# Raw rows by feature for the key and query products, a reordered first gather, and on-chip node sums for the last chunk of a graph-transformer layer

## The chip, the cores and the metric

The kernel runs on one core of a Trainium2 chip. The metric is device time in microseconds (us) of one execution. A core has TensorE (PE: matmuls, with the weight loads PEld beside them), VectorE (DVE), ScalarE (ACT), GpSimd (POOL), SyncE (SP), and 16 DMA engines. SP, ACT and POOL issue DMAs, each from its own in-order instruction queue. All data is 32-bit float, and in the trace each 128x512 product is two matmul instructions.

## The reference, cut to what matters

N = 10,000 nodes with D = 512 features, 160,000 edges sorted by destination, 8 heads of 64.

```python
xn = layernorm(x)
gnn = relu(segment_sum((xn @ W)[src] * edge_w[:, None], dst) + bias)
q, k, v = split(xn @ w_qkv.T)
q = softmax(q, over the 64 of a head) / 8 ; k = softmax(k, over all nodes)
mix = gamma_layernorm(((k^T v per head) applied to q) @ w_out.T)
x = x + gnn + mix
x = x + experts(layernorm(x))      # 2-matmul FFN, hidden 6*341, top-2 router on the mean row
```

## The kernel before, in words

The nodes are cut into `NCH` = 20 chunks: 19 of 512 rows (128 partitions x `SUB` = 4) and a last one of 272 rows (68 x 4). There are four stages.

**Early stage (0 to 160 us, chunks 0 and 1).** `normal_rows` (L411) loads each chunk of x on SP (L416), takes row statistics on DVE (`row_stats`, L166 and L167) and 1/std on POOL (L169, L171), normalises on ACT (L422) and writes the result to `xn_d` in HBM on ACT's queue (L424). The first two chunks stay in SBUF (`KEPT`), the others go through 7 buffers. After `LISTS` = 10 chunks the edge lists are loaded (L446 to L451), and from then on two steps of `place_edges` (L454 on, all on DVE) run for each chunk normalised. Meanwhile PE does the key and query products of chunks 0 and 1 (`times`, L209), into which `work` (L698) threads more `normal_rows`.

**Keys stage (160 to 1236 us, chunks 2 to 19).** For each chunk: `turned_rows` (L837) turns the normalised rows with 16 PE transposes (`transposed`, L201) that ACT and DVE copy out of PSUM (L203) into `xnT`, which has one buffer; DVE forms four sums `xs_b` (L226 to L229); `seven` (L246, its products at L243) makes keys and queries by a seven-product scheme; ACT takes exponents (L896 to L901), scaled by `usable` (1.0 while the weights are small enough); DVE does the query softmax (L192 to L194); PE adds keys^T times rows into the context (`pc`, L911) and turns the queries (L201), which ACT writes to HBM. The rows for `pc` are read back from `xn_d` by SP (L834).

**Edges, threaded through the keys and the attention stage.** Edges lie in 1250 tiles of 128. For each tile POOL gathers the 128 source rows by an indirect DMA into one of 24 `msg` buffers (L583). Tiles go in 217 groups (`NQ`), of 8 tiles and later of 4. A visit of a group (`edges_summed`, L595) is 16 or 8 matmul instructions with a 0/weight matrix (L601), an ACT copy (L604), and a write of partial node sums to `part_d` in HBM (L605). `work(us)` adds a model cost and visits groups up to that cost divided by `PACE`. The stage starts at minus 16 tiles' worth (L862). `carry` (L673) joins neighbouring windows in HBM by an accumulating DMA on POOL. `gathered(c)` (L1013) gathers chunk c's node sums from `part_d`, forcing enough groups first (`far_enough`, `AT_HAND`).

**Attention stage (1297 to 2143 us).** For each chunk: queries times mix (`po`, L209), layer norm, 16 transposes of the node sums `at` (L201) into `aT`, and the product with the graph weights (`pg`, L209), with bias and relu on DVE (L1089, L1090). PE's order is written out by hand. At chunk 17 (`c == NCH - 3`) `all_edges_in` visits the last six groups, carries, and gathers the sums of chunks 18 and 19; then come `po` of chunk 19 and `pg` of 17, 18 and 19.

**Experts stage (2143 us to the end).** The FFN (L243) over 20 chunks. Its first product needs rows of chunk 0 read back (L328), normalised (ACT L351), turned (DVE L367) and summed (`xs`, L233 to L236). `sums_of_weights` (L226 to L229 on 1280 elements) prepares its weights in chunk 17.

Of the kernel before, what the change touches and what calls it, by code (L numbers as in the profile page):

```python
# [17 lines left out]
P = 128  # L18
# [11 lines left out]
ROWS_IN = 1.6  # L30
LISTS = 10
# [6 lines left out]
MIXED = 3  # L38

AT_HAND = [(5, 320), (7, 384), (8, 424), (9, 472), (10, 520), (11, 560), (12, 604), (13, 640), (14, 680), (15, 716), (16, 752),  # L40
           (17, 788), (18, 820)]
# [13 lines left out]

@with_exitstack
def gps_layer_kernel(
    ctx: ExitStack,
    tc: tile.TileContext,
    x: bass.AP,  # L60
    src: bass.AP,
# [40 lines left out]

    const = ctx.enter_context(tc.tile_pool(name="const", bufs=1))
# [33 lines left out]
    stats2 = const.tile([P, NCH, SUB, 2], F32, name="stats2")  # L137

# [10 lines left out]
    ZERO_ROW = NQ * P  # L149
# [38 lines left out]
    def softmax_rows(q, r, s):  # L188

        q3 = q[:r, s, :].rearrange("p (h e) -> p h e", e=HEAD)  # L190
        qs = small.tile([P, D // HEAD], F32, name="qs")
        nc.vector.tensor_reduce(qs[:r], q3, axis=AX.X, op=ALU.add)  # L192
        nc.vector.reciprocal(qs[:r], qs[:r])
        nc.vector.tensor_tensor(q3, q3, qs[:r, :, None].to_broadcast([r, D // HEAD, HEAD]), ALU.mult)  # L194
# [29 lines left out]
    def sums_of(o, a11, a12, a21, a22):  # L224
# [4 lines left out]
        nc.vector.tensor_tensor(o[3], a12, o[1], ALU.subtract)  # L229
# [149 lines left out]
    def sums_of_weights():  # L379
        w1_sb, w1_sum = held_w["w1"], held_w["w1_sum"]  # L380
        p_half, q_half = slice(0, PAIRS * P), slice(PAIRS * P, 2 * PAIRS * P)
        sums_of([w1_sum[:, i] for i in range(4)], w1_sb[:, :KH, p_half], w1_sb[:, KH:, p_half],
# [5 lines left out]
    with ExitStack() as ph:  # L388
# [17 lines left out]

        normal = []
        placing = []
        last_stats = [None]

        def normal_rows(n):  # L411

            for c in range(len(normal), min(len(normal) + n, NCH)):
                r = chunks[c][1]
                xt = (xp if c < KEPT else a_io).tile([P, SUB, D], F32, name="xn")
                nc.sync.dma_start(xt[:r], tokens(x, c))  # L416
                mv = small.tile([P, SUB, 2], F32, name="mv")
# [10 lines left out]
                for _ in range(2 if placing else 0):  # L428
                    next(placing[0], None)
# [3 lines left out]
        nc.scalar.dma_start(part_d[ZERO_ROW : ZERO_ROW + P, :], zero)  # L433
        normal_rows(2)
# [8 lines left out]
        n_odd = ep.tile([1, 1], I32, name="n_odd")  # L443

# [9 lines left out]
        def place_edges(dst_sb, row_sb):  # L454


            nc.vector.tensor_scalar(row_sb, row_sb, 2, None, op0=ALU.arith_shift_right)
            yield
# [40 lines left out]
            nc.vector.scalar_tensor_tensor(place, place, float(SUB), good, op0=ALU.add, op1=ALU.subtract)  # L499
            yield  # L500
# [23 lines left out]
        def window_at(node, more):  # L524
            tile_no = NET * (node / N) ** 0.5 + more
            return min(max(int(tile_no / 2 if tile_no < 2 * PAIRED else tile_no - PAIRED), 0), NW)

        def span(c):
            return window_at(chunks[c][0], -SPARE), window_at(chunks[c][0] + SUB * chunks[c][1], SPARE)

        def spans_hold():
            for c, (b, r) in enumerate(chunks):
                for i, w, op, edge in ((0, span(c)[0], ALU.is_le, b), (1, span(c)[1], ALU.is_ge, b + SUB * r)):
                    at = 3 + len(AT_HAND) + 2 * c + i
                    nc.vector.tensor_scalar(count[:, at : at + 1], bases[:, w : w + 1], float(edge // SUB), None, op0=op)
# [37 lines left out]
        def edges_in(i):  # L573
# [4 lines left out]
            for j in range(batch):  # L578
                for h in range(GROUP):
                    k = h * batch + j  # L580
                    if k < n:
                        m[k] = pools["m"].tile([P, D], F32, name="msg")
                        nc.gpsimd.indirect_dma_start(  # L583
# [11 lines left out]
        def edges_summed(i, batch, m, sel):  # L595
# [7 lines left out]
            part = pools["w"].tile([P, D], F32, name="part")  # L603
            nc.scalar.copy(part, pm)  # L604
            nc.scalar.dma_start(part_d[i * P : (i + 1) * P, :], part)  # L605
# [5 lines left out]

        def squares_of(w, tag):
            sq = b_io.tile([P, KB, D], F32, name="sq", tag=tag)
            nc.scalar.activation(sq, w, AF.Square)
            return sq
# [19 lines left out]
        def oddities():  # L635
# [8 lines left out]
            nc.vector.tensor_tensor(n_odd, n[:, 0:1], n[:, 1:2], ALU.add)  # L644

# [30 lines left out]
        carried = []  # L676
        for i in range(PARTS):
# [7 lines left out]
        ahead = [AHEAD]  # L685
        EARLY_TOTAL = PRODUCT * KB * ROWS_IN * 3 * KB

# [10 lines left out]
        def work(us):  # L698
# [6 lines left out]
            edges_to(groups_of(int(done[1] / pace[0])))  # L705

        in_order = ph.enter_context(ExitStack())
        in_order.enter_context(tc.manual_schedule(engines={mybir.EngineType.PE}))
# [11 lines left out]
        def all_edges(fp):  # L720
# [12 lines left out]
            nc.vector.tensor_copy(row_of, four)  # L733
            dst_sb = fp.tile([P, NET], I32, name="dst_far")
# [95 lines left out]
        def rows_of(c):  # L830
# [3 lines left out]
            nc.sync.dma_start(xn[: chunks[c][1]], tokens(xn_d, c))  # L834
            return xn

        def turned_rows(c, xn):  # L837
            xnT = b_io.tile([P, KB, SUB * P], F32, name="xnT")
            transposed(xnT, xn, chunks[c][1], psum, "ps", by_act=range(KB) if c < EARLY else (1, 3))
            return xnT  # L840

        def finish(o, ek, r, at):
            if o is ek:
                nc.vector.tensor_tensor(kacc[:r], kacc[:r], ek[:r, at, :], ALU.add)
            else:
                softmax_rows(o, r, at)

        wk = kvp.tile([P, KB, D], F32, name="wk")
        nc.sync.dma_start(wk, w_qkv_t[:, D : 2 * D].rearrange("(k p) d -> p k d", p=P))
        nc.sync.dma_start(wq, w_qkv_t[:, :D].rearrange("(k p) d -> p k d", p=P))  # L850
        squared = [squares_of(wk, "qT"), squares_of(wq, "xs_b")]
# [3 lines left out]
        xnT = turned_rows(0, xn)  # L855
        for c, (_, r) in enumerate(chunks):
            if c == EARLY:
                for _ in placing[0]:
                    pass
                norm_ctx.close()  # L860
                pools["w"] = edge_ctx.enter_context(tc.tile_pool(name="edge_w", bufs=3))
                done[1] = -16 * PACE  # L862
# [8 lines left out]
            if c < EARLY:  # L871
                for o, w in ((ek, wk), (qt, wq)):
                    sums = []
                    for s in range(SUB):
# [4 lines left out]
                        if c == s == 0 and o is ek:  # L879
                            norms(0, squared[0])  # L880
                            norms(1, squared[1])
                            as_they_are()
                        for i, po in enumerate(sums):
                            at = s + 1 - len(sums) + i
                            nc.scalar.activation(o[:r, at, :], po[:r], AF.Exp, scale=usable[:r])
                            finish(o, ek, r, at)
                        sums = []
            else:
# [4 lines left out]
                for s in range(SUB // 2):  # L893
                    first = seven(ek, qt, s, r, xnT, xs, (wk, wq), kq_sum, lambda n: work(n * KH * PRODUCT))
                    s2 = s + SUB // 2
                    nc.scalar.activation(ek[:r, s, :], first, AF.Exp, scale=usable[:r])  # L896
# [576 lines left out]
```

## Time and profile before

| what | value |
|---|---|
| median of 3 runs (lowest to highest) | 3510.95 us (3510.28 to 3531.97) |
| the profiled execution's own time | 3518.48 us |
| its span, first to last instruction | 3516.7 us |
| PE busy, PEld busy | 3256.7 us (93%), 1916.0 us (54%) |
| DVE, ACT, POOL busy | 1766.5, 831.1, 1311.2 us |
| mean granted TensorE clock | 0.961 |
| HBM read, written | 491.21 MB, 166.63 MB |

A line of instruction groups reads: source line, engine, operation, output<-inputs, shapes, count | busy us, mean ns of one | idle time of the engine just before them, and what ended most of it. In a timeline the first two numbers are the start and the duration in us, and a bracket is the engine's idle time ahead of the instruction and its releaser; "issue" means that the profile shows no releaser. In a view of windows each row is a stretch of the span, with each engine's busy time in it (and its number of instructions), the granted PE clock, the busy share of the DMA engines, and GB/s.

### The profile page before, as it was taken

To read this page: it belongs to the slowest core of one execution; us is meant where nothing else is said; L and a number is where in the kernel's file an instruction comes from. 1 tells how busy PE (TensorE), PEld (TensorE's weight loads), DVE (VectorE), ACT (ScalarE), POOL (GpSimd) and SP (SyncE) were. 2 spreads that over 40 slices of the span, in tenths; PEclk is the share of its full clock that TensorE was granted. 3 is DMA by queue.
4 is the path that set the end of the run, shared out by engine and by line. 5 is a ranking of instruction groups with operands and counts; after the bars stand their busy time and mean duration, and the time that the engine had idled before them with its cause. 6 is when DMAs were issued, how large, how long until landed. Compare 5 with 4: busy or idle time off the path is not lost. (4 is left out here: it accounts for less than half of the span.)

```text
span 3516.7 us, 36142 instructions
## 1 busy us (share of the span) xinstructions
PE 3256.7 (93%) x12819; PEld 1916.0 (54%) x12819; DVE 1766.5 (50%) x3902; ACT 831.1 (24%) x1674; POOL 1311.2 (37%) x1421
## 2 busy tenths in 40 slices
PE   6899998988999989898998988999999999999998
PEld 3433333333333333333333335888888888888886
DVE  6644445444444425564565557445445544544542
ACT  5321212121112112121222113222222222222221
POOL 3466666665666656676676630000000000000000
PEclk8999999999999979899999988999999999999999
DMA  9677777776777878898998882221212212122111
GB/s 392 235 217 249 227 247 248 254 223 208 227 223 243 247 275 318 313 332 293 318 336 301 294 268 61 60 75 58 60 57 76 60 49 84 49 60 73 60 37 38
DMA packets 216735, 654.39 MB, mean 186 GB/s; under 512 B 34425, under 2 KB 74361, under 8 KB 188831
## 3 DMA queue, kind: packets, MB, share of 16 engines
q0 software_dynamic: 104096, 354.29, 32.0%
q1 hardware_dynamic: 69992, 175.33, 15.2%
q10 hardware_dynamic: 42452, 122.31, 9.0%
q8 instruction: 105, 1.72, 0.2%
q14 instruction: 90, 0.74, 0.1%
HBM read 491.21 MB, written 166.63 MB: 187 GB/s over the span
## 5 line engine op out<-in xcount | busy, mean ns | idle before, releaser
L583 POOL DMA_INDIRECT msg<-xn_d,src_sb x1250 | 1229.9, 984 | 634.4 <-issue 287.2
L601 PE MATMUL pm<-msg,sel 128*32 128x512 f32 x2504 | 351.7, 617 | 54.5 <-issue 44.5
L911 PE MATMUL pc<-xn,ek 128*128 128x512 f32 (+1 forms) x640 | 306.5, 624 | 20.5 <-issue 15.0
L209 PE MATMUL po<-G,qT 128*128 128x512 f32 (+1 forms) x640 | 302.0, 613 | 13.0 <-issue 12.2
L209 PE MATMUL pg<-wq,aT 128*128 128x512 f32 (+1 forms) x640 | 301.3, 617 | 10.2 <-issue 9.0
L604 ACT COPY part<-pm 128x512 f32<-128x512 f32 x217 | 127.1, 586 | 733.9 <-PE pm L601 276.0
L601 PEld LDWEIGHTS pm<-msg,sel 128*32 128x32 f32 x2504 | 66.1, 110 | 302.7 <-issue 266.2
L209 PEld LDWEIGHTS pg<-wq,aT 128*128 128x128 f32 (+1 forms) x640 | 117.7, 192 | 195.7 <-issue 184.7
L911 PEld LDWEIGHTS pc<-xn,ek 128*128 128x128 f32 (+1 forms) x640 | 122.7, 199 | 177.4 <-issue 164.7
L209 PEld LDWEIGHTS po<-G,qT 128*128 128x128 f32 (+1 forms) x640 | 117.4, 191 | 185.6 <-issue 181.4
L243 PE MATMUL px<-xnT,w_sb 128*128 128x256 f32 (+1 forms) x800 | 204.6, 379 | 6.8 <-DVE u L1290 6.8
L243 PE MATMUL p<-kq_sum,xs_b 128*128 128x512 f32 (+1 forms) x432 | 201.4, 600 | 3.2 <-issue 2.4
L166 DVE BATCH_NORM_STATS2 st<-ot 128x6 f32<-128x512 f32 (+1 forms) x160 | 110.3, 689 | 178.5 <-issue 119.2
L243 PE MATMUL px<-w_sb,hh 128*128 128x256 f32 (+1 forms) x800 | 185.7, 379 | 0.0
L243 PE MATMUL py<-xs,w_sum 128*128 128x256 f32 (+1 forms) x800 | 185.3, 374 | 0.0
L243 PE MATMUL p<-wk,xnT 128*128 128x512 f32 (+1 forms) x288 | 148.1, 637 | 34.9 <-issue 26.7
L243 PE MATMUL py<-w_sum,hh 128*128 128x256 f32 (+1 forms) x800 | 179.2, 379 | 0.0
L589 DVE TENSOR_TENSOR sel<-iota_w,place 128x128 f32<-128x128 f32 (+2 forms) x217 | 74.5, 344 | 206.1 <-remote 86.2
L243 PEld LDWEIGHTS px<-xnT,w_sb 128*128 128x128 f32 x800 | 150.7, 192 | 29.9 <-DVE u L1290 10.0
L243 PEld LDWEIGHTS py<-w_sum,hh 128*128 128x128 f32 (+1 forms) x800 | 150.0, 188 | 22.7
L243 PEld LDWEIGHTS px<-w_sb,hh 128*128 128x128 f32 (+1 forms) x800 | 150.0, 188 | 22.7
L243 PEld LDWEIGHTS py<-xs,w_sum 128*128 128x128 f32 x800 | 149.8, 190 | 19.9
(298 smaller groups left out, 4577.4 us busy)
## 6 DMA issues: line engine op xcount, KB each, us to landing
part_d<-part ACTq DMA_DIRECT2D x217, 256.0 KB
msg<-xn_d,src_sb POOLq DMA_INDIRECT x1250
xn<-in_x SPq DMA_DIRECT2D x19, 1024.0 KB
xn_d<-xn ACTq DMA_DIRECT2D x19, 1024.0 KB
qT_d<-qT ACTq DMA_DIRECT2D x19, 1024.0 KB
qT<-qT_d SPq DMA_DIRECT2D x19, 1024.0 KB
xt<-in_x SPq DMA_DIRECT2D x19, 1024.0 KB
x_d<-ot SPq DMA_DIRECT2D x19, 1024.0 KB
```

Of the source, the lines that this page charges most:

```text
L166: nc.vector.bn_stats(st[:r, s, :], t[:r, s, :])
L209: nc.tensor.matmul(po[:r, :], t[:, kb, s * r : (s + 1) * r], w[:, kb, :], start=kb == 0, stop=kb == KB - 1)
L243: nc.tensor.matmul(o, lhs[j], rhs[j], start=start and j == 0, stop=stop and j == n - 1, skip_group_check=True)
L583: nc.gpsimd.indirect_dma_start(out=m[k], out_offset=None, in_=xn_d, in_offset=bass.IndirectOffsetOnAxis(ap=src_sb[:, t0 + k : t0 + k + 1], ...
L589: nc.vector.tensor_tensor(sel[:, :n], iota_w[:, None, :].to_broadcast([P, n, WIN]), place[:, t0 : t0 + n, None].to_broadcast([P, n, WIN]), ...
L601: nc.tensor.matmul(pm[h * WIN : (h + 1) * WIN, :], sel[:, k, :], m[k] if k < len(m) else m[0], start=j == 0, stop=j == batch - 1, skip_gro ...
L604: nc.scalar.copy(part, pm)
L911: nc.tensor.matmul(pc, ek[:r, s, cb * P : (cb + 1) * P], xn[:r, s, :], start=s == 0, stop=s == SUB - 1)
```

## The change

1. **Raw rows by feature.** The program gets a second input `x_t`: x laid out so that a chunk's rows, turned, are one contiguous run per partition. `xnT` is loaded from it by SP, raw, in place of the transposes. Centring is moved to the weights (`centred`: each column of wk and wq loses its mean over the input features), and the row's 1/std becomes the scale of the exponent (`rate` for chunks 0 and 1, `rates` after).
2. **Early stage.** wk, x_t of chunk 0 and wq are issued ahead of all x rows. `LISTS` is 18 and the placing of edges is put behind the last row statistics; `place` itself is put behind chunk 1's query softmax. The reload of chunk 2 goes behind the last load of x. `ROWS_IN` is 2.0. The keys stage starts at minus 11 tiles' worth.
3. **End of the edges.** The last six groups (211 to 216, `ON_CHIP` = 211) stay in SBUF as `parts`. The sums for chunk 19 are products of `parts` with 0/1 matrices (`numbered`, `last_sums`), in two portions: groups 0 to 3 of the six after `pg` of chunk 17, the rest, and the gathered rows, ahead of `pg` of chunk 19. `po` of chunk 19 moves up to chunk 16; edges are visited up to group 214 while chunk 17 is multiplied.
4. **Start of the experts.** The load of chunk 0's rows moves to chunk 17; its normalising and turning stay in chunk 18, now ahead of `sums_of_weights`; and chunk 19's bias additions are put behind these weight sums.

```diff
-ROWS_IN = 1.6
-LISTS = 10
+ROWS_IN = 2.0
+LISTS = 18
...
+        def turned_rows(c):
+            xnT = b_io.tile([P, KB, SUB * P], F32, name="xnT")
+            nc.sync.dma_start(xnT[:, :, : SUB * chunks[c][1]], columns(x_t, c))
+            return xnT
+
+        def centred(w):
+
+            pcol = psum.tile([P, D], F32, name="pcol", tag="ps")
+            for kb in range(KB):
+                nc.tensor.matmul(pcol, all_ones, w[:, kb, :], start=kb == 0, stop=kb == KB - 1)
+            for kb in range(KB):
+                nc.vector.scalar_tensor_tensor(w[:, kb, :], pcol, -1.0 / D, w[:, kb, :], op0=ALU.mult, op1=ALU.add)
...
+        wk = kvp.tile([P, KB, D], F32, name="wk")
+        nc.sync.dma_start(wk, w_qkv_t[:, D : 2 * D].rearrange("(k p) d -> p k d", p=P))
+        xnT = turned_rows(0)
+        nc.sync.dma_start(wq, w_qkv_t[:, :D].rearrange("(k p) d -> p k d", p=P))
+        squared = [squares_of(wk, "qT"), squares_of(wq, "xs_b")]
+        centred(wk)
         normal_rows(2)
...
-            nc.sync.dma_start(xn[: chunks[c][1]], tokens(xn_d, c))
+            load = nc.sync.dma_start(xn[: chunks[c][1]], tokens(xn_d, c))
+            if c == KEPT:
+                behind(load, last_load[0])
...
-                for _ in placing[0]:
-                    pass
+                for step in placing[0]:
+                    if step:
+                        behind(step, last_softmax[0])
+                rates = ep.tile([P, NCH, SUB], F32, name="rates")
+                nc.vector.tensor_scalar(rates, stats1[:, :, :, 1], usable, None, op0=ALU.mult)
...
-                done[1] = -16 * PACE
+                done[1] = -11 * PACE
...
-                    nc.scalar.activation(ek[:r, s, :], first, AF.Exp, scale=usable[:r])
+                    nc.scalar.activation(ek[:r, s, :], first, AF.Exp, scale=rates[:r, c, s : s + 1])
...
                 normal_rows(NCH)
+                behind(next(placing[0]), last_stats[0])
                 xn_next = rows_of(c + 1)
             if c + 1 < NCH:
-                xnT = turned_rows(c + 1, xn_next)
+                xnT = turned_rows(c + 1)
...
-            nc.scalar.dma_start(part_d[i * P : (i + 1) * P, :], part)
+            if i < STORED:
+                nc.scalar.dma_start(part_d[i * P : (i + 1) * P, :], part)
...
+        def numbered():
+            b, r = chunks[-1]
+            mine = io.tile([P, NQ - ON_CHIP + 1, SUB, r], F32, name="mine", tag="xt", bufs=1)
+            number = mine[:, NQ - ON_CHIP]
+            nc.gpsimd.iota(number, pattern=[[1, SUB], [SUB, r]], base=b, channel_multiplier=0,
+                           allow_small_or_imprecise_dtypes=True)
+            for g in range(NQ - ON_CHIP):
+                nc.vector.tensor_scalar(mine[:, g], number, node_of[:, g : g + 1], None, op0=ALU.is_equal)
+            return mine
...
+                for g in groups:
+                    nc.tensor.matmul(pt, parts[g // 3][:, g % 3, kbs], mine[:, g].rearrange("p s n -> p (s n)"),
+                                     start=g == groups[0], stop=at is None and g == groups[-1], skip_group_check=True)
...
-            if c == NCH - 3:
-                all_edges_in()
-                ats += [gathered(c + 1), gathered(c + 2)]
...
-            if c + MIXED < NCH - 1:
+            if c + MIXED < NCH:
                 mixed.append(attention(c + MIXED, nodes_rows))
-            elif c == NCH - 3:
-                mixed.append(attention(NCH - 1, nodes_rows))
-            else:
-                nodes_rows()
+            elif c < NCH - 1:
+                nodes_rows()
+            else:
+                last_sums(aT, mine, range(FIRST_SUMS, NQ - ON_CHIP), at)
...
+                if c == NCH - 1:
+                    behind(added, weights_summed)
...
             if c == NCH - 3:
-                sums_of_weights()
+                mine = numbered()
+                aT_last = io.tile([P, KB, SUB * P], F32, name="aT_last", tag="ot", bufs=MIXED + 2)
+                edges_to(limit[0])
+                last_sums(aT_last, mine, range(FIRST_SUMS), None)
+                rows_first = all_edges_in()
             if c == NCH - 2:
...
-                turn = turned_in(0, rows_turned(0, xn))
+                turn = turned_in(0, rows_turned(0, rows_first))
+                weights_summed = sums_of_weights()
```

## The prediction

> **What bounds the kernel now.** I read the page first, then the windows by stage, PE's waits in each stage, and timelines where these waits are long. Windows (columns: stretch, length, busy us of PE, PEld, DVE, ACT, POOL, then clock, DMA share, GB/s):
>
> ```profile
> 0.00:160.00 160.00, 111.43 (x339) 58.98 (x340) 105.78 (x301) 81.48 (x117) 52.75 (x102) 0.86 0.80 318
> 160.00:1236.00 1076.00, 985.35 (x3551) 399.95 (x3550) 500.33 (x1002) 208.46 (x337) 698.15 (x717) 0.96 0.75 235
> ...
> 2020.00:2143.00 123.00, 93.35 (x322) 37.77 (x322) 81.18 (x182) 24.52 (x56) 34.05 (x74) 0.87 0.76 229
> 2143.00:3516.60 1373.60, 1351.62 (x6146) 1145.85 (x6145) 660.44 (x1338) 360.71 (x866) 0.00 (x0) 0.99 0.19 58
> ```
>
> PE bounds the keys stage (92% busy) and the experts (98%), which the change leaves alone. The weak stretches are the first 160 us and the 123 us ahead of the experts. PE's timeline shows what they wait for:
>
> ```profile
> 31.72 5.91 PE L209 MATMUL pk<-wk,xnT 128*128 128x512 f32 x8 [13.29 <-ACT xnT L203]
> ...
> 100.73 0.47 PE L201 MATMUL pt<-ident,qt 128*128 128x128 f32 x1 [13.32 <-DVE G L918]
> ...
> 159.87 1.88 PE L243 MATMUL p<-kq_sum,xs_b 128*128 128x512 f32 x4
> ...
> 2142.57 2.04 PE L243 MATMUL px<-xs,w_sum 128*128 128x256 f32 x4 [13.68 <-DVE xs L235]
> ```
>
> The first product starts only at 31.7 us, behind load, statistics, normalising, transposes and copies. At 87 to 100 PE waits for DVE, which does statistics and the placing of edges together. At the end 13.7 us pass until the experts' first operand is ready. In the keys stage the 16 transposes of rows stand between products:
>
> ```profile
> 419.49 1.92 PE L601 MATMUL pm<-msg,sel 128*32 128x512 f32 x16
> 421.34 1.97 PE L201 MATMUL pt<-ident,xn 128*128 128x128 f32 x16
> 423.15 7.03 PE L911 MATMUL pc<-xn,ek 128*128 128x512 f32 x16
> ```
>
> Start to start they take 423.15 - 421.34 = 1.81 us of PE. POOL is the second resource, as the page's groups and POOL's timeline show:
>
> ```profile
> L583 POOL DMA_INDIRECT msg<-xn_d,src_sb x1250 | 1229.9, 984 | 634.4 <-issue 287.2
> ...
> 149.77 1.26 POOL L583 DMA_INDIRECT msg<-xn_d,src_sb  x1 [13.24 <-DMA xn_d<-xn]
> 151.33 0.96 POOL L583 DMA_INDIRECT msg<-xn_d,src_sb  x1 [0.30 <-issue]
> ```
>
> A gather costs POOL 0.975 us (mean in the keys stage) plus 0.30 us: 1.275. Its 716 gathers there take 913 of 1076 us, 85%. POOL starts at 149.8, when the last normalised rows have landed. SP's timeline tells why so late: chunk 19's load is issued at 114.33, behind the reload of chunk 2 at 113.89, which had held SP since 91.8.
>
> **What the Trainium skill says.** "TensorE: Matmul & The Clock Gate", Part 1: the PE clock falls to half after an idle window of about 3.4 us and needs sustained work to rise. The trace agrees: the clock is 0.86 and 0.87 in the two stretches with long waits, 0.99 in the experts; so a removed wait returns more than its length. The same page, Part 4: a PE transpose ends in PSUM and needs a copy; here these are the L203 copies, about 0.6 us on ACT and 0.69 on DVE. "DMA: Bandwidth & Descriptors", "Issuing engines are not separate DMA queues": all queues share 16 engines and interleave, so rows loaded by SP share with POOL's gathers. Whether that hurts is seen below.
>
> **Early stage.** From 31.7 to 159.9 are 128.2 us: products of two chunks 4 x 13.7 = 54.9, `pc` 4 x 7.03 = 28.1, weight norms about 9, five sets of transposes about 1.8 each = 9; together 101. Waits of 5.9, 13.3 and some short ones make 21; the rest, 6 to 7, is half clock. Two of those sets turn rows and go (-3.6; the set of chunk 0 lies ahead of 31.7). Centring adds 2 x 8 matmul instructions, at the warm pace of 13.7/32 = 0.43 us 3.4 us each, about double when cold, and 4 DVE operations of about 0.69 us (as L1090, also 512 columns with PSUM), of which the first product needs one. The new start: two 1 MB loads issued at 0.82 were ready at 7.5 and 10.7 us; wk and x_t of chunk 0 take their place, so centring can begin at 6 to 8, takes 7 cold, and the first product starts near 15: 16.7 us earlier. For wq centring costs 3.4 + about 3 of waiting. Of the 13.3 us wait I let two thirds go, as the placing (about 22 us of DVE in the trace: 1.4 to 1.5 for each pass over 1250, 0.6 to 1.0 for each over 866) is now behind the statistics. Sum: -16.7 - 3.6 + 6.4 - 8.5 = -22; I take chunk 2 at 137, a gain of 23. The placing then falls at 110 to 140 on a DVE that also owes 6.5 us of softmax, 4.9 of `kq_sum` and 2.8 of `xs_b`. If all of placing stands before `xs_b`, 10 to 15 us of the gain are lost; if the waits go entirely, up to 12 more come. Bounds: 8 to 35. SP's queue: three 1 MB loads ahead of the x rows delay these by 1 MB net, about 2.6 us at the page's 392 GB/s; the last row no longer waits until 114, so gathers start near 125 to 135. The first visit comes at 19 tiles x 0.9 = 17 us after chunk 2's start, at 154; eight gathers take 10 us. That is enough.
>
> **Keys stage.** Gone from PE: chunks 3 to 19, 16 x 1.81 + 1 = 30 us. The four copies for each chunk go with them, off two engines that were not the limit. Added: a 1 MB load for each chunk on SP, of which only the landing matters. `xnT` is free at 419.5 in the chunk shown (last reading product) and is next needed at 446.4; less 1.8 removed and 2.8 for the DVE sums, 22 us remain for a load that took 7 to 10 us at the start beside others. So it is hidden, with about 12 us of cover. Does it slow the gathers? Windows of 20 us in which 2 MB of other transfers pass show no fewer gathers (POOL column):
>
> ```profile
> 400.00:420.00 20.00, 17.94 (x56) 6.43 (x58) 9.43 (x18) 4.77 (x8) 13.22 (x14) 1.00 0.68 202
> ...
> 440.00:460.00 20.00, 20.00 (x70) 7.70 (x69) 6.88 (x20) 1.89 (x3) 13.87 (x16) 1.00 0.90 312
> ```
>
> But POOL's share goes from 85% to 913/1046 = 87%, and PE waited 29.1 us before `p`, up to 5.3 us at a time, mostly with no releaser shown. I read that as visits that overtook their gathers, so a third of the gain is given back: 20 us. Bounds 0 (gathers set the pace) and 30. `rates` in place of `usable` is one per-partition scale for another: nothing. `nodes_on_chip` is some 17 tiny DVE operations of about 0.15 us in chunk 5, hidden: DVE is 47% busy.
>
> **End of the edges.** From 2020.4 to 2142.6 are 122 us: work 86, waits 1.4+2.5+3.3+3.7+5.1+13.7 = 29.7, half clock about 6. In the new order `po` of chunk 19 stands among the visits, which take 10 groups x 1 us as before but with 7 to 14 us between most of them, while POOL needs 4 x 1.275 = 5.1 us a group: the 16 us of waits at visits shrink to about 3. Added on PE: 4 x 6 x 2 instructions of 272 columns, at 0.25 us (2.0 us for 8 in the row of `ph` at 272) 12 us, and about 2 for adding chunk 19's gathered rows, less its 1.2 of transposes: +13. The gathered sums of chunk 18 need the carry: before, 2075.9 to 2094.6, 19 us, plus about 4 for the part write. From group 213's visit PE has 3 x 3.4 + 1 + 8 + 2 = 21 us of other work: a wait of about 3. The experts' operands are made while chunk 19 is multiplied (8 + 14 us of PE): ACT 6.3, DVE 2.3 + 2.8, weight sums 5.9 make 17 after the statistics product, so the 13.7 us go, bar 2. Sum: 86 + 13 + 3 + 3 + 2 + 2 = 109, a gain of 13; bounds 3 and 22.
>
> **Sum.** 23 + 20 + 13 = 56. The profiled execution, 3518.5 (span 3516.7), would become 3462; it stands 7.5 above the median, 3511, so the comparable figure is **3455**.
>
> **Rivals.** *Gathers set the pace*: the keys stage returns nothing and the start loses 7: gain 16 + 0 + 13 = 29, 3482. For: 85% POOL, the waits at visits; against: 163 us of POOL slack in the stage. *The early stage is bound by rows and DVE*: DMA share is already 0.80, two more MB and the placing stand before chunk 2: gain 8 + 20 + 13 = 41, 3470. *The waits go too*: 35 + 30 + 22 = 87, 3424. *Slower*: the single `xnT` buffer. If the raw load lands later than the 22 us, every chunk waits, and PE turns cold; at 22 + 3.3 us (56/17) all gain is spent, at 27 us the time is 3511 - 56 + 17 x 5 = 3540. Against it stands the 7 to 10 us. *That it doesn't do what it says* is excluded for the transposes: no code is left that turns rows.
>
> **How the numbers follow.** Forecast 0.58, gathers 0.14, early stage 0.13, waits too 0.10, slower 0.05. About 1% (35 us) can be told from no change: faster 0.58 + 0.13 + 0.10 = 0.81, within 0.14, slower 0.05. The range 3424 to 3490 holds all but the slower case and half of the deeper one; the likeliest's own is 3440 to 3470.
>
> **What would show it.** Right: no transposes of `xn` in the keys stage; first `pk` near 15 us, first keys product near 137, first gather before 140; the keys stage near 1056 us; no 13 us wait ahead of `px`. Wrong: waits on `xs_b` or on DMA `xnT`; POOL above 90% with longer waits at `pm`; DVE waits between 110 and 160 us.

## The result, and the profile after

The changed kernel takes 3546.23 us (median of 7 runs, 3529.85 to 3559.18), the kernel before in the same comparison 3518.30 (7 runs, 3507.34 to 3531.97). The ratio is 1.0082, with a 95% interval from 1.0056 to 1.0108: slower by 28 us, where the forecast was 56 us faster. The profiled execution took 3539.64 us, span 3537.9. Stage times below are of one profiled execution each, while executions of one kernel spread by 25 to 29 us here, so a difference of a few us between two profiles shows little by itself.

Windows of the changed kernel, cut at its own stage boundaries (columns as in the prediction):

```profile
0.00:172.40 172.40, 114.85 (x306) 58.53 (x307) 113.16 (x329) 76.47 (x107) 39.40 (x97) 0.82 0.77 308
172.40:1273.20 1100.80, 970.88 (x3310) 375.81 (x3309) 483.08 (x972) 191.39 (x305) 719.05 (x736) 0.94 0.78 251
1273.20:1309.80 36.60, 18.93 (x101) 11.15 (x99) 7.57 (x22) 2.93 (x5) 16.10 (x17) 0.72 0.81 273
1309.80:2160.10 850.30, 794.00 (x2720) 308.48 (x2721) 481.00 (x1218) 175.54 (x346) 529.72 (x573) 0.95 0.87 297
2160.10:3537.90 1377.80, 1351.71 (x6147) 1146.09 (x6145) 669.24 (x1362) 360.44 (x867) 0.00 (x0) 0.99 0.20 60
```

Boundaries in both profiles are the first keys product, the last `pc`, the first `po` and the first `px`. The kernel before had 159.9, 1087.7, 38.5, 856.5 and 1374.1 us in the same five stretches. So the early stage lost 12.5, the keys stage 13.1 and the experts 3.7; the middle gained 1.9 and the attention stage 6.2: +21 us together, the difference of the two spans. PE's timeline of the changed kernel, at the places shown before:

```profile
15.86 1.55 PE L224 MATMUL pk<-wk,xnT 128*128 128x512 f32 x3 [0.85 <-DVE wk L465]
...
80.43 0.45 PE L216 MATMUL pt<-ident,qt 128*128 128x128 f32 x1 [10.24 <-DVE stats L182]
...
155.57 0.45 PE L216 MATMUL pt<-ident,qt 128*128 128x128 f32 x1 [15.80 <-DVE qt L209]
...
172.45 1.88 PE L258 MATMUL p<-kq_sum,xs_b 128*128 128x512 f32 x4
...
2160.13 1.03 PE L258 MATMUL px<-xs,w_sum 128*128 128x256 f32 x4
...
2170.36 2.08 PE L258 MATMUL px<-xnT,w_sb 128*128 128x256 f32 x4 [4.88 <-DVE u L1379]
```

The first product starts at 15.9 us as forecast, partly by luck: centring began at 9.6 us, not at 6 to 8, and took 5.4, not 7. The 13.7 us wait ahead of `px` is gone. But PE waits for the query softmax twice: 24 us in four waits at chunk 0's transposes (80 to 96 us), 20.6 in four at chunk 1's (156 to 162). Behind the first `px` stands a new wait of 4.88. DVE's timeline tells why chunk 1's softmax is late:

```profile
125.46 1.28 DVE L181 BATCH_NORM_STATS2 st<-xn 68x6 f32<-68x512 f32 x2 [14.69 <-DMA xn<-in_x]
...
128.73 0.78 DVE L500 TENSOR_SCALAR row_sb<-row_sb 128x1250 int32<-128x1250 int32 x1
...
145.30 0.69 DVE L241 TENSOR_TENSOR xs_b<-xnT 128x512 f32<-128x512 f32 x1
...
151.81 0.68 DVE L207 TENSOR_REDUCE qs<-qt 128x8 f32<-128x512 f32 x1
```

DVE sits idle for 14.7 us for the last chunk's rows, then runs the placing that was put behind them, chunk 2's sums and one `kq_sum`, and only at 151.8 the softmax (143.25 in a profile of the kernel before). POOL's group and timeline:

```profile
L622 POOL DMA_INDIRECT msg<-xn_d,src_sb x1250 | 1229.3, 983 | 669.6 <-issue 300.5
...
145.77 1.35 POOL L622 DMA_INDIRECT msg<-xn_d,src_sb  x1 [14.11 <-issue]
173.11 0.96 POOL L622 DMA_INDIRECT msg<-xn_d,src_sb  x1 [25.99 <-DVE count L553]
```

A message is the gather of one tile's 128 rows. The second one waits 26 us for the last step of the placing; by the program, the message buffers lie in memory that the placing's scratch held until then. The first visit follows at 191.4.

Chunk 2 takes 66.3 us, not 50.4, and one wait makes the difference. Lines of the changed kernel's timelines of PE, ACT and DVE ("remote" stands for a releaser that the profile does not tell):

```profile
217.37 3.78 PE L967 MATMUL pc<-xn,ek 128*128 128x512 f32 x4 [17.81 <-ACT ek L951]
215.20 0.59 ACT L648 COPY part<-pm 128x512 f32<-128x512 f32 x1 [21.51 <-remote]
215.21 0.42 DVE L628 TENSOR_TENSOR sel<-iota_w,place 128x256 f32<-128x256 f32 x1 [22.26 <-remote]
```

PE waits for exponents, and ACT and DVE both stand still until 215.2, although the visit that ACT is to copy ended at 193.3. What held them is not shown. On other chips the same kernel has no such wait and chunk 2 takes 45.7 us (`after_again` below).

Chunks 3 to 19 take 1037.3 us before and 1034.5 after. PE's gaps there sum to 89.6 us before and 111.7 after. While the granted clock is one half, half of the time is lost: 44.2 us before and 54.6 after. What is left as work is 903.5 and 868.2: the transposes did go (-35.3), and waits (+22.1) and the lower clock (+10.4) took back 32.5.

### The profile page after: what moved, and what is told of

Same layout as the page of the kernel before. It is cut to its first block, busy times and chain, and to the rows that moved or that the text cites. A ratio compares the mean times of both kernels' runs of the same rounds, so it can differ in the third digit from the quotient of the medians.

```text
span 3537.9 us, 35613 instructions
## 1 busy us (share of the span) xinstructions
PE 3250.4 (92%) x12579; PEld 1900.1 (54%) x12579; DVE 1754.0 (50%) x3901; ACT 806.8 (23%) x1630; POOL 1304.3 (37%) x1423
## 4 chain that ended last, share of the span: by engine, by line
PE 56%; DMA 3%; DVE 2%; issue 2%; another core or an unknown queue 0%; ACT 0%; DVEq 0%; SPq 0%
PE px L258 14%; PE pz L258 10%; PE py L258 9%; PE po L224 8%; PE pg L224 7%; PE pm L640 4%; PE ph L258 2%; DMA z_d<-xt 1%; PE pt L216 1%; DMA xt<-x_d 1%; DMA w_sb<-in_w 1%; DMA x_d<-ot 0%; DVE xt L1441 0%; DVE st L181 0%
## 5 line engine op out<-in xcount | busy, mean ns | idle before, releaser
L224 PE MATMUL pg<-wq,aT 128*128 128x512 f32 x608 | 284.1, 612 | 7.4 <-issue 4.6
L224 PEld LDWEIGHTS pg<-wq,aT 128*128 128x128 f32 x608 | 112.0, 193 | 180.8 <-issue 162.5
L181 DVE BATCH_NORM_STATS2 st<-ot 128x6 f32<-128x512 f32 (+1 forms) x160 | 110.0, 688 | 155.5 <-issue 109.6
L258 PEld LDWEIGHTS px<-xnT,w_sb 128*128 128x128 f32 x800 | 150.7, 192 | 34.7 <-DVE u L1379 14.9
```

The lines of the kernel that those rows point to most:

```text
L181: nc.vector.bn_stats(st[:r, s, :], t[:r, s, :])
L224: nc.tensor.matmul(po[:r, :], t[:, kb, s * r : (s + 1) * r], w[:, kb, :], start=kb == 0, stop=kb == KB - 1)
L258: nc.tensor.matmul(o, lhs[j], rhs[j], start=start and j == 0, stop=stop and j == n - 1, skip_group_check=True)
```

## The experiments

The runs fell on several chips, of two kinds: on kind A the kernel before takes 3518 to 3533 us, on kind B 3297 to 3301. The result above is of kind A. Expectations that name a time were often written for the other kind than the one that the run fell on; ratios and stages are compared then. Ratios are to the kernel before on the same chip. "Chunks" is the time of chunks 3 to 19; stages are from the profiles.

**The parts alone (kind B).** `old_placing` is the changed kernel with the old schedule of the placing:

```diff
-LISTS = 18
+LISTS = 10
...
+                for _ in range(2 if placing else 0):
+                    next(placing[0], None)
...
-                    if step:
-                        behind(step, last_softmax[0])
...
-                behind(next(placing[0]), last_stats[0])
```

> The changed kernel with the placing of the edges as in the kernel before: the lists at chunk 10, two placing steps beside each further chunk's statistics, no wait behind the last statistics or the last softmax. Theory L (the late placing holds the gathers back, because the messages' buffers lie where its scratch lay): gathers run without a break from about 150 us, not 173; keys start near 157 and chunk 2 takes 50 us, not 66; time near 3520, some 27 us under the changed kernel and the same as the kernel before. Rival R (the early stage is set by loads of rows, the placing is only what happens to stand there): keys start stays near 170, chunk 2 stays over 60, time 3540 to 3550. Rival S (an earlier chunk 2 only moves its wait to later chunks): chunk 2 near 50, but chunks 3 to 19 together over 1045 us against 1034, time 3535 to 3545.

1.0039 (1.0025 to 1.0053). Messages run from 154.7 without a break and chunk 2 takes 45.7 us, but the keys still start at 172.7. L is right on the messages and wrong on the start. The changed kernel itself measured 1.0073 (1.0051 to 1.0095) on the same chip at another time, so the late placing likely accounts for part of the loss: chunks take 884.9 here and 896.2 there.

`tail_only` is the kernel before with parts 3 and 4 alone (also the reload of chunk 2 behind the last load, and the added steps of `nodes_on_chip`).

> The kernel before with only the last part of the change: the last chunk's node sums by a product, edges end a chunk sooner, its early loads and placing at the end. The forecast on record gives this part -13 us: 3505. Theory from the changed kernel's trace: the 13.7 us wait ahead of px is gone, but 25 us of tensor work are added to the attention stage, 4.9 us of a new wait for DVE stand behind the first px, and the loop's other waits shrink by 12 only: -3 to -8 us, 3510 to 3515. Rival: the sum is a loss once nothing else hides it, 3520 to 3530.

1.0023 (1.0012 to 1.0035): a small loss, as the rival said. Against a profile of the kernel before on this chip the attention stage takes 808.6 for 807.8 us, the experts 1381.1 for 1373.3. In the attention stage PE's waits fall from 31.3 to 17.8, and its busy time rises from 776.5 to 790.8, as the added instructions ask (12.1 us for the products with `mine`, 4.0 for adding the gathered rows, less 1.2 that go: 14.9). The wait ahead of `px` turned into one behind it, and PE has three new waits for DVE, 9.4 us together, around chunk 17's product. DVE's and PE's timelines of `tail_only`:

```profile
1852.18 0.36 DVE L1076 TENSOR_SCALAR mine<-mine,node_of 128x272 f32<-128x272 f32 x1 [17.54 <-POOL mine L1073]
1853.20 1.12 PE L214 MATMUL pt<-ident,at 128*128 128x128 f32 x4 [6.35 <-DVE ot L1172]
...
1924.94 1.03 PE L256 MATMUL px<-xs,w_sum 128*128 128x256 f32 x4
...
1935.16 2.07 PE L256 MATMUL px<-xnT,w_sb 128*128 128x256 f32 x4 [4.88 <-DVE u L1369]
```

POOL makes the numbers in `mine` (part 3's `numbered`) only behind 15 messages that it issues without a break. DVE stands 17.5 us at their first use, with the relu that PE waits for behind it. The whole change has the same wait of DVE on this chip, 17.54 us (`after_again`).

`keys_rows` is the kernel before with only the raw columns of chunks 2 to 19; the weights are centred before the first product, chunks 0 and 1 turn their rows as before:

```diff
         def turned_rows(c, xn):
             xnT = b_io.tile([P, KB, SUB * P], F32, name="xnT")
+            if c >= EARLY:
+                nc.sync.dma_start(xnT[:, :, : SUB * chunks[c][1]], columns(x_t, c))
+                return xnT
...
```

> The kernel before with only this of the change: from chunk 2 on the keys and queries are computed from raw columns loaded from x_t, with the centred weights and the rates; chunks 0 and 1, the placing and the end stay as before. The forecast on record gives this -20 us (30 us of row transposes gone, a third given back): near 3498. Theory G (in the keys stage the edges' messages set the pace, not TensorE): chunks 3 to 19 take 1030 to 1037 us as in both kernels, tensor work falls by 35 us and waits plus half clock rise by as much: 3510 to 3520. Rival X (the columns' megabyte a chunk slows the messages): 3525 to 3540.

1.0037 (1.0022 to 1.0051). Chunks: 883.4, and 882.2 in the kernel before, 883.4 in `tail_only`: thirty microseconds of PE work are gone and nothing comes back, as Theory G said. And the keys start 9 us later, at 168.7, though chunks 0 and 1 are as before. DVE's timeline of `keys_rows`:

```profile
150.64 0.69 DVE L233 TENSOR_TENSOR xs_b<-xnT 128x512 f32<-128x512 f32 x1 [11.46 <-DMA xnT<-in_x_t]
...
153.05 1.27 DVE L199 TENSOR_REDUCE qs<-qt 128x8 f32<-128x512 f32 x2
```

The columns' load of chunk 2 is issued at 138.9, when chunk 1's last products have read the single `xnT` buffer, and lands at 150.6. DVE has `xs_b` ahead of chunk 1's softmax, so the softmax waits for a load that it does not need.

`no_xt` loads the columns for chunks 0 to 2 only; later keys and queries are of the wrong rows.

> The changed kernel with the columns loaded for chunks 0 to 2 only; the later chunks reuse those of chunk 2, so keys and queries of chunks 3 to 19 are computed from the wrong rows, with the same instructions on the engines. It takes away 17 MB of loads. Theory G (messages set the pace by their own issue and landing): chunks 3 to 19 fall by at most 6 us from 1034, time 3538 to 3546. Rival X (the columns' loads contend with the messages and give the 30 us back): chunks 3 to 19 at 1005 to 1020, time 3515 to 3530.

1.0113 (1.0095 to 1.0130), chunks 901.7. No gain shows. Why it is slower than the changed kernel I do not know, so it could hide one; the pace of the messages, below, is the better evidence that the columns' loads do not slow them.

**Which resource (kind B).** `before_again` and `after_again` are the two kernels unchanged; `slower_visits` is `old_placing` with `PACE = 0.95`; `half_after` gathers every other message of the paired tiles:

```diff
-                    if k < n:
+                    if k < n and j:
+                        m[k] = m[k - 1]
+                    elif k < n:
```

> The kernel before, unchanged, for its profile on the chip that the others of this call run on. In the call before, kernels close to it took 51.4 us a chunk of the keys stage with next to no wait on TensorE, where its first profile shows 58 us with waits. Theory P (a chip or an execution where the waits are absent: tensor work sets the chunk): chunks of 51.4 us, keys start near 160, end near 3300. Rival: chunks of 58 us and end near 3520 as in its first profile.

> The changed kernel, unchanged. Theory P (issue of messages on GpSimd, 1.254 us each, sets the keys stage once the row transposes are gone: its end stands 945 to 950 us after gathers run without a break): gathers break off from 146 to 172 us as in the kernel without the columns' loads, keys stage ends near 1120, time 3320 to 3335, some 0.8 per cent over the kernel before. Rival (the waits of its first profile are the kernel's own): chunks of 60 us, time over 3500.

> The changed kernel with the placing of the kernel before, and edges' visits spread over 5.5 per cent more of the keys stage's work (0.95 us of counted work a tile, not 0.9: 38 tiles a chunk for 40); the visits left over come in the attention stage. Theory P: 38 messages of 1.254 us are 47.7 us, under the chunk's tensor work of 49.2, so waits for messages go, chunks 3 to 19 fall from 885 to some 840 to 850, attention grows by 8 to 12: time 3275 to 3290, under the kernel before. Rival (messages don't set the pace): keys as in the kernel with the old placing less the moved visits, attention longer by as much, 3310 to 3320.

> The changed kernel in which, for the tiles in pairs (the keys stage's), only the first message of each pair is gathered and stands for both; the second half's sums are of wrong rows, with the same tensor work. Theory P: no wait for messages is left in the keys stage, chunks 3 to 19 at 49.5 us, some 845 together, whatever the gathers' start. Rival: chunks unchanged, 885 to 905 together or over 1000 where the first profile's waits return.

`before_again`: one run of 3296.94 us; 51.4 us in most chunks, no PE wait. `after_again`: 1.0073 (1.0051 to 1.0095), a loss like that on kind A; early stage +10.3, keys stage +12.4, middle -0.7, attention stage -12.1, experts +5.6. Inside the keys stage it is another loss: chunk 2 takes 45.7 us, 1.5 less than before, and chunks 3 to 19 take 896.2, 14.0 more. `slower_visits`: chunks 842 as Theory P said, but the attention stage 857.1, where `after_again` has 795.7, so the time missed: 1.0075 (1.0058 to 1.0092). There PE waits 32.3 us for messages in 29 places. The messages moved and their time moved with them. `half_after`: one run of 3263.90 us, chunks 855.4, most of them 49.7 to 49.8.

**The same half on both kernels (kind B, one chip), and on kind A.**

> The kernel before in which, for the tiles in pairs (the keys stage's), only the first message of each pair is gathered and stands for both; the second half's sums are of wrong rows, with the same tensor work. Theory P: on a chip with chunks of 51.4 us next to nothing changes in the keys stage (880 us for chunks 3 to 19, TensorE sets it); on one with chunks of 60 us they fall to 51 to 53, if the messages' number is the cause. Rival (the slow chip's waits come from elsewhere): chunks stay near 60.

> The changed kernel with the same half of the messages left out, beside the one above. Theory P: chunks 3 to 19 some 25 to 32 us shorter than half_before's, since with the messages out of the way the row transposes' 30 us come back. Rival (the columns' loads or the rest of the change cost as much): within 10 us of half_before's.

> The changed kernel with half of the keys stage's messages left out (sums of wrong rows, same tensor work), once more. If the chip is one where the kernel before takes about 3520: theory M (messages cause the waits there: 40 a chunk[...]) says chunks of 50 to 52 us; the rival (waits that the chip has whatever the messages) says over 57. On a chip where the kernel before takes about 3300 it repeats the earlier look: 49.8 us a chunk, 3256 to 3264.

Chunks: `half_before` 875.5, `half_after_again` 856.8. With the messages out of the way 18.7 us of the transposes' 30 come back, under Theory P's 25 and over the rival's 10; 49.8 us a chunk for 51.4. What is missing is mostly in one chunk: chunk 18 takes 55.5 for 50.7, and in it DVE waits 7.98 us for the columns of the last chunk. Five windows of 215 to 1030 us, each of one kernel, show what POOL does meanwhile (the fifth column of busy time; its instructions are messages but for at most one carry). `before_again`:

```profile
215.00:1030.00 815.00, 815.00 (x3186) 344.74 (x3185) 449.29 (x894) 188.82 (x303) 615.71 (x628) 1.00 0.83 271
```

`after_again`:

```profile
215.00:1030.00 815.00, 808.50 (x2897) 320.24 (x2899) 425.44 (x849) 169.33 (x268) 617.47 (x631) 1.00 0.87 292
```

`half_before`:

```profile
215.00:1030.00 815.00, 815.00 (x3186) 344.66 (x3185) 450.10 (x895) 188.81 (x303) 325.52 (x321) 1.00 0.54 172
```

`half_after_again`:

```profile
215.00:1030.00 815.00, 811.25 (x3001) 326.23 (x3000) 437.48 (x878) 173.48 (x275) 338.84 (x329) 1.00 0.61 199
```

The changed kernel's first profile, on kind A:

```profile
215.00:1030.00 815.00, 732.79 (x2528) 287.10 (x2529) 367.32 (x742) 145.10 (x231) 534.30 (x547) 0.96 0.78 255
```

On kind B POOL issues 627 and 631 messages in 815 us before and after: one each 1.30 and 1.29 us, of which 0.98 is busy and 0.30 a gap; 99% of the gaps between two messages are this short one. A chunk's visits are 80 instructions, 40 messages: 40 x 1.29 = 51.7 us. That is what the chunk took before (51.4 of PE work), so PE and POOL were level, and taking 1.8 us of PE work from a chunk leaves POOL. POOL's column of busy time reads 76%; with the 0.30 us gap it is full. The pace is the same with the columns' loads as without, so these don't slow it.

PE's column falls by only 6.5 us, to 808.50, though its transposes are gone, because its waits for messages lie inside the visits. PE's group of visits in the same window, of `before_again`, `after_again` and `half_after_again`:

```profile
L601 PE MATMUL pm<-msg,sel 128*32 128x512 f32 x1280 | 153.9, 598 | 0.0
L640 PE MATMUL pm<-msg,sel 128*32 128x512 f32 x1268 | 177.5, 599 | 6.5 <-DMA msg<-xn_d,src_sb 6.4
L642 PE MATMUL pm<-msg,sel 128*32 128x512 f32 x1312 | 157.7, 598 | 0.0
```

A visit takes 1.92 us. In `after_again` 20 of the 80 visits are stretched; in the other two none is.

On kind A one message takes 1.51 us before and 1.49 after, and there POOL is not full: 45 and 54 longer gaps, 142 and 129 us of the 815, end mostly when PE frees a buffer. The reckoning by POOL's issue holds for kind B alone.

`half_after_slow` fell on kind A (3339.42 us in one run, 3532.85 for the kernel before beside it): its chunks are 857.6 together, 49.7 to 49.8 us most of them, as on kind B. Its attention stage, where no message is left out, takes 852.0, as long as in the changed kernel's first profile. So the waits of these chunks hang on the messages on kind A too. Halving them takes away POOL's issues, transfers and pressure on the 24 buffers at once; which of these counts on kind A it does not tell. PE's waits in the changed kernel on kind A, and then in `half_after_slow`, 215 to 1030 us (columns: line waited at and releaser, us in total, times, longest):

```profile
PE p L258 <- issue: 30.8, 11, 5.3
PE pc L967 <- ACT ek L951: 22.0, 3, 17.8
PE p L258 <- ACT u L291: 13.7, 4, 6.6
```

```profile
PE pc L969 <- DVE G L972: 3.4, 1, 3.4
```

**Repairs.** `softmax_first` is `keys_rows` with one order more on DVE:

```diff
+                for inst in sums_of([xs[:, i, :, :h] for i in range(4)], ...
+                    if c == EARLY:
+                        behind(inst, last_softmax[0])
```

`softmax_first_pace` has `PACE = 0.92` besides, `softmax_first_late` starts at minus 32 tiles, and `before_pace` is the kernel before with `PACE = 0.92`.

> The kernel before with raw columns for the keys stage only (as in the earlier run of that part), and on DVE the sums of chunk 2's columns put behind chunk 1's last softmax, so that the wait for their load no longer stands ahead of it. Theory W (those 11.5 us of DVE, with the softmax behind them, are the early stage's loss): query transposes of chunk 1 run near 141 to 149 us as in the kernel before, the keys start near 160, not 168.7. Theory P adds: the keys stage ends where the messages let it, first gather plus some 947 us, so of these 8 us little reaches the end: 3306 to 3312. Rival to P: all 8 are kept, 3300 to 3304. Rival to W: keys start stays over 166.

> The same with 0.92 us of counted work a tile, not 0.9: 39.1 messages a chunk, 49.0 us of GpSimd against 49.7 of TensorE. Theory P: chunks 3 to 19 lose their waits for messages and fall to 850 to 860; 15 messages go to the attention stage, which waits for messages too and grows by 10 to 20: 3293 to 3305, a draw with the kernel before at best. Rival (attention has room for them): 3275 to 3285.

> The same with 0.9 us a tile and the first visit 16 tiles of work later: 16 messages fewer are needed by the end of the keys stage, and each visit has 14 us more of lead. Theory P: chunks 3 to 19 at 850 to 862 without waits for messages but for the last, attention longer by 10 to 20: 3293 to 3306. Rival (attention has room): 3275 to 3285.

> The kernel before with 0.92 us of counted work a tile, for comparison: TensorE sets its keys stage, not the messages, so 15 visits only move. Theory P: keys 3 to 4 us shorter, attention longer by as much or by up to 20 where it waits for messages: 3300 to 3316. Rival (later visits help by themselves): under 3295.

All on kind A: 0.9969 (0.9953 to 0.9984), 1.0065 (1.0046 to 1.0084), 1.0047 (1.0030 to 1.0065) and 1.0111 (1.0083 to 1.0139). Theory W holds; DVE's timeline of `softmax_first`:

```profile
140.88 1.27 DVE L199 TENSOR_REDUCE qs<-qt 128x8 f32<-128x512 f32 x2
...
151.70 0.69 DVE L233 TENSOR_TENSOR xs_b<-xnT 128x512 f32<-128x512 f32 x1 [0.89 <-DMA xnT<-in_x_t]
```

The load lands at the same time, the softmax no longer stands behind it, and the keys start at 155.5: 13 us before `keys_rows`, 4 before the kernel before. Where the rest of the 11 us that its median gains comes from is not shown. Later visits only lose, and Theory P's chunks without waits did not come on kind A: they take 1035.3 and 1045.2 us in `softmax_first_pace` and `softmax_first_late`, 1039.0 in `softmax_first`, and the attention stage is 35 to 40 longer. In `before_pace` the attention stage takes 902.1, not 856.5, the last message is issued 62 us later than in the first profile of the kernel before, and the keys stage, too, takes 26 us more, which neither theory has and which stays unexplained.

> The kernel with raw columns for the keys stage and the softmax first, and one edit more: on SP's queue the reload of chunk 2's rows, which waits for chunk 0's products, is put behind the last chunk's load of rows, which stands behind it in the kernel before. Theory P (messages bind from their first to the end of the keys stage, and on a slow chip to the last): the last rows' statistics come near 118 us, not 129, the first message near 138, not 151, and the end of the keys stage moves by 8 to 13 us: 0.3 to 0.4 per cent under softmax_first, 0.5 to 0.8 under the kernel before. Rival (the first message's time is hidden): within 0.1 per cent of softmax_first.

> The kernel with raw columns for the keys stage and the softmax first, for comparison on this chip. On a chip where chunks take 51 us (before near 3300): 3300 to 3306, as messages bind the keys stage's end. On a chip where they take 60 (before near 3530): 0.3 per cent under the kernel before, as it measured.

The edit of `rows_then_reload` is part 2's `behind(load, last_load[0])` alone. On one chip of kind B: 1.0001 (0.9992 to 1.0010) and 1.0004 (0.9995 to 1.0013). The first message is issued at 133.5 instead of 150.9 and nothing follows. The rival is right, and my rule "947 us after the first message" falls: the 24 buffers are full after 24 messages, and the next waits 15.75 us for a visit, so an earlier start is not kept. `softmax_first` is level with the kernel before here.

`after_mended` is `old_placing` with the same order on DVE.

> The changed kernel with the placing of the kernel before, and on DVE the sums of chunk 2's columns behind chunk 1's last softmax. Chunk 0's products still start near 16 us. Theory W: the keys start falls from 172.7 to 155 to 160, as far as in the kernel with raw columns in the keys stage alone (155), so that the early start of chunk 0 is worth nothing more, since the last rows' statistics and normalising (129 to 144 us) stand behind the loads of rows. Rival V (the early start is worth its 16 us once nothing stands ahead of the softmax): 140 to 150. The time, theory P (GpSimd issues 40 messages a chunk at 1.29 us, 51.7 us, whatever TensorE does): the keys stage ends within 10 us of the kernel before's; the last part's 8 us stay lost in the experts: 0.1 to 0.4 per cent over the kernel before. Rival: under it by 0.3 per cent.

Kind A, 1.0007 (0.9988 to 1.0026): both repairs together return the change's loss. The keys start at 167.6, earlier than 172.7 but later than both theories' numbers, so 8 us of Theory W are not reached: DVE has three of the `kq_sum` between the softmaxes there. The keys stage ends at 1241 (1248 in the first profile of the kernel before), as Theory P said; the loss that it puts in the experts does not show (1374.9 us, 1374.1 there). Rival V is out, and PE shows why: chunk 1's first product starts at 115.0, at 112.2 in `softmax_first`, which starts chunk 0 11 us later. Chunk 0's query transposes wait for DVE in four places, 32 us in sum, and give the early start back.

## Why the prediction was wrong, by its steps

**Early stage, forecast -23, came +12.5.** The start near 15 us was right, the centring in sum too. Wrong was the term "of the 13.3 us wait I let two thirds go". The wait was put down to the placing; it is the softmax standing among the row statistics, which wait for loads, and it grew to 24 us; PE had arrived there earlier (first `pc` at 63 us, 80 in the kernel before). DMA share is 0.77 in this stretch, and the last rows' statistics come at 125, near the 129 of before. The rival "bound by rows and DVE" was the right one in kind, though it still gave a gain of 8; its mechanism came twice, as placing ahead of `xs_b` and as `xs_b` ahead of the softmax (shown by `softmax_first`). I had priced the single `xnT` buffer in the keys stage, where PE did not wait for it, and not at chunk 2, where the load could be issued only at 132.9. The Trainium skill, "DMA: Bandwidth & Descriptors", section "Issuing engines are not separate DMA queues", says that queues share the engines; no cost of the columns' loads to the messages shows here (one each 1.30 and 1.29 us on kind B), only the wait of their own consumer.

**First message at 125 to 135, came 145.8, and the second 173.1.** I followed the placing on DVE, not the memory of its scratch, where the message buffers come to lie. `old_placing` shows that part: messages without a break, and chunks 11 us shorter than in `after_again`.

**Keys stage, forecast -20, came +13.1**, of which +15.9 is chunk 2 and -2.8 chunks 3 to 19. Chunk 2's part is the one wait of 17.8 us in which ACT and DVE stood still; no term of the forecast had it, and its cause stays open. The removed work was sized right (30 forecast, 35 in the profile). The term "a third is given back" failed: all but 2.8 us was. I had both numbers, 1.275 us a message and 716 messages, and made of them a busy share of 85% with "163 us of slack". The comparison that decides on kind B is by chunk: 40 messages against the work of one chunk, 51 to 52 us each. On kind A, where the forecast was scored, the stage's waits hang on the messages too (`half_after_slow`), but not on POOL's issue alone, which left 129 us of 815 free. The rival "gathers set the pace" was right in that the stage returns nothing; it gave 3482, since it kept the gains at both ends. The result lies in the case "slower" (chance 0.05), but its mechanism did not come: PE waits nowhere in the keys stage for `xs_b`, and the single `xnT` buffer cost its time at chunk 2's softmax and at the last chunk's columns.

**End of the edges, forecast -13, came -6.2 in the attention stage, -1.9 in the middle and +3.7 in the experts.** The 13.7 us wait went, and PE's added work was sized nearly right (13 forecast, 14.9 by its groups). What failed is the sum of the waits that were to be left, "3 + 3 + 2": 4.88 came back behind the first `px`, and on kind B 9.4 stood at DVE, behind the numbers that POOL makes. How the attention stage's -6.2 on kind A splits further is not shown. Alone the part loses (`tail_only`).

**The Trainium skill**, "TensorE: Matmul & The Clock Gate", Part 1, says that idle time lowers the PE clock, and I used it for what a removed wait returns. The trace agrees, but with the other sign: with 22.1 us of new waits in chunks 3 to 19 the lost clock grew by 10.4.

Open: what in the messages makes every engine wait on kind A. With half of them the waits of chunks 3 to 19 are gone; which resource they fill there was not found. The packets of the messages' DMA queue last as long on both kinds (a mean of 173 and 167 ns in the kernel before, 215 to 1030 us), so slower packets alone do not explain it. Chunk 2's wait stays open with it: with half of the messages it is 9.3 us on kind A.

## What to carry to other kernels

Before work is credited on one engine, count what the next resource must do in the same chunk, with its mean time from start to start rather than its busy time, and compare the two per chunk; on kind B they were level at 51.5 us. Of a load that takes the place of computed data, ask not only whether it is hidden but which instruction waits for it and what stands behind that instruction on its in-order engine. Work moved later also holds its memory longer: look up who gets that memory next.

## What the runs showed that I had not expected

The same kernel takes 3518 to 3533 us on some chips and 3297 to 3301 on others, at clocks of 0.96 and 0.985. With 384 of the 1250 messages left out the changed kernel took 40 us less than the kernel before on kind B (3258.3 beside 3298.7) and 193 less on kind A (3339.4 beside 3532.9). On kind A ACT's copy of a visit's sums starts a median of 4.4 us after the visit's last matmul in the keys stage of the changed kernel, on kind B 0.14, and with half of the messages 0.14 on kind A too.
